# MLP second layer of a fused attention and cluster block: seven quarter products in place of eight, their sums on GpSimd, the first layer's sums in the scores' banks

## The chip, the cores and the metric

One NeuronCore of a Trainium2 chip runs the whole program. The metric is the device time of one execution in microseconds (us). All data is float32. TensorE makes each float32 product in two passes, so the profile counts two MATMUL records, and two weight loads (PEld), for each product in the code.

## The reference: what is computed

There are four images of 256 channels by 64 x 64 = 4096 pixels. Each goes through two layers.

Layer 0 is self-attention over the 4096 pixels: `q` and `k` have 32 channels, `v` has 256, `attn = softmax(q k)`, and `x = gamma * (v attn^T) + x`.

Layer 1 is a cluster block: a group norm over the whole image, two 1x1 convolutions to 96 channels, a similarity of each pixel to four centres in each fold, and a projection back to 256 channels that is added to x. Then comes the part that matters here:

```
hdn = conv1x1(group_norm(y), mlp_w1, mlp_b1)           # 256 -> 1024 channels
hdn = conv1x1(gelu(hdn), mlp_w2, mlp_b2)               # 1024 -> 256 channels
y   = y + ls2 * hdn
z   = relu(batch_norm(y * dw_w))
out = relu(batch_norm(conv1x1(z, pw_w)))               # 256 -> 256 channels
```

## The kernel before, in words

**Stages.** For each image b the program writes attention's `weighting` (64 units of 128 x 4 key rows against 512 pixels; `sc` are the scores, `av` the sums with v), then `cluster`, then `mlp`. The order of the instructions on each engine is that of the code: nothing is reordered, and only waits on data and on buffers decide when an instruction starts. Work of the next image fills gaps: its projections (vp, kp, qp) fill `cluster`, and eight of its scores are made inside `mlp`, one in each block, since ScalarE must copy them out of their banks.

**Banks.** TensorE writes to eight banks of 512 columns. Pool `ps_s` has two pairs of banks (tag "s": scores, pw, and others), `ps_a` two single banks (a0, a1: the sums of the second layer), `ps_m` two single banks (tag "m"). A tile that takes a bank waits until all that read the tile before it there are done.

**MLP.** Line 1118 on. An image's 4096 pixels are eight blocks of 512 (`blocks`; image 2 does seven here and leaves the last one to be done as filling work in image 3's cluster stage, `late_block`). A block has four steps j. `first(nb, j)` makes 2 x 128 hidden rows (rows j and j + 4 of 128, called lo and hi) for 512 pixels from 2 x 128 input rows, which are 2 x 2 quarters times 2 x 2 quarters. It does so with **seven** products of 256 columns (Winograd's form of Strassen's scheme) and seven sums: products A, abcd, CD, bac, B, D, bcd (called by their weights, line 1197), sums `plus` by VectorE from the bank and the tile `hs` (line 1233), a copy of A's product by ScalarE (line 1236), gelu by ScalarE (line 1226). The factors of the input are made by `norm`: two scalings by VectorE (line 1146) and four sums by GpSimd (lines 1159 to 1163). `hs` has four quarters of 128 x 256: h1 and h2 are lo for the first and second half of the pixels, h3 and h4 are hi.

`second(nb, acc, hs, j)` adds the second layer's part of step j: four products of 512 columns (line 1204) into the banks a0 and a1, that is **eight** quarter products. It is a generator: `mo(n)` in the following `first` draws n of its products between the products of the first layer, so the products of step j are issued in step j + 1.

After a block's last step, `finish` adds the two banks to y, scaled (VectorE, line 1277), and puts the relu of each half (ScalarE, line 1267) on the list `hooks`, which `hook()` empties in the next `first`, after the first sum. `last`, after step j = 1 of the next block, makes the closing layer's product pw (line 1173) in a pair of banks, and its two output activations (line 1183) are hooked into the step after. A score (line 359) is made after step j = 2: the copy of its first half (line 367) is issued at once, that of the second half (line 368) is hooked, and its maxima (line 372, VectorE) are drawn one by one by `rest`.

**Attention.** A dictionary `at` says after which unit and quarter a score is made (`due`), with a lead of ten units. In image 0, unit 0 has two scores, before and after its last two quarters' products.

Of the kernel before, what the change touches and what calls it, by code (L numbers as in the profile page):

```python
# [8 lines left out]
F32 = mybir.dt.float32  # L9
# [4 lines left out]
P = 128  # L14
# [31 lines left out]
def attention_then_cluster_block(  # L46
# [224 lines left out]
    def attention(b, xs):  # L271
# [281 lines left out]
        def maximum():  # L553
            half["dg"] = across(0, "rden")

# [6 lines left out]
        if b:  # L562
            for i in range(6):
                del at[i, 0]
            at.update({divmod((14 * i + 10) // 5, RG): GRP + i for i in range(8)})
        else:
            at[0, 2], at[0, 0] = at[0, 0], GRP + 1

# [7 lines left out]
        def weighting(ahead, fill, early):  # L576
# [3 lines left out]
            for u in range(units):  # L580
# [15 lines left out]
                elif u == units - 1:  # L596
                    turn_mlp()
                if u == 0 and not b:
                    weigh(u, av, 0)
                    weigh(u, av, 1)  # L600
                due(u, 0)
                if p - units > 1:
                    ahead()
                if g == GRP - 1 and more:
                    exps(u + 1)
                if u or b:
                    weigh(u, av, 0)
                    due(u, 1)
                    weigh(u, av, 1)
                if nb:  # L610
# [509 lines left out]
    def mlp(b, ys, stats2, fill, nxt, blocks):  # L1120
# [10 lines left out]
        nc.gpsimd.tensor_tensor(w_bac, w_abcd, W_D, ALU.add)  # L1131
        nc.gpsimd.tensor_tensor(w_bcd, W_B, w_abcd, ALU.subtract)
        ga, gb = group_norm(b, "gn2", stats2, fill)
        fill(N)
        ob = out[b].rearrange("(k p) h w -> p k (h w)", p=P)
        pairs = {}
# [3 lines left out]
        def norm(nb, eng):  # L1140
# [17 lines left out]
            scaled(0)  # L1158
            eng.tensor_tensor(f, f, e, ALU.subtract)  # L1159
            scaled(1)  # L1160
            eng.tensor_tensor(t2, h, f, ALU.subtract)
            eng.tensor_tensor(t3, e, t2, ALU.subtract)
            eng.tensor_tensor(t4, t2, g, ALU.subtract)

# [25 lines left out]

        norm(0, nc.vector)
        if nxt:
# [3 lines left out]
        def product(out, w, j, x):  # L1196
            nc.tensor.matmul(out, w[:, j * P : (j + 1) * P], x, start=True, stop=True)  # L1197

        def second(nb, acc, hs, j):

            for i in range(2):
                jj = j + HID // P // 2 * i
                for c in range(KC):
                    yield nc.tensor.matmul(  # L1204
                        acc[c],
                        w2_s[:, jj, c * P : (c + 1) * P],
                        hs[:, i],
                        start=(j == 0 and i == 0),
                        stop=(j == HID // P // 2 - 1 and i == 1),
                    )  # L1210

        def first(nb, j, todo):
# [5 lines left out]
            h1, h2, h3, h4 = quarters(hs)  # L1218
            u = ps_m.tile([P, NB], F32, tag="m", name=f"hu_{b}_{nb}_{j}")[:, :HB]
            p = ps_m.tile([P, NB], F32, tag="m", name=f"hp_{b}_{nb}_{j}")[:, :HB]  # L1220
            q = ps_s.tile([P, 2, NB], F32, tag="s", name=f"hq_{b}_{nb}_{j}")[:, 0, :HB]
            act = AF.Gelu_apprx_tanh
# [4 lines left out]

            def mo(n):
                for _ in range(n):
                    next(todo, None)  # L1230

            def plus(dst, ps, term):
                nc.vector.tensor_tensor(dst, ps, term, ALU.add)  # L1233

            product(p, W_A, j, e)
            nc.scalar.copy(h1, p)  # L1236
# [3 lines left out]
            rest(2 if nb == blocks - 1 and j == 3 else 1)  # L1240
            mo(1)
            product(q, W_CD, j, f)
            product(u, w_bac, j, t3)
            plus(h3, u, h2)
            product(p, W_B, j, g)
            plus(h4, q, h3)
# [3 lines left out]
            gelu(h1, h1, lo)  # L1250
            mo(1)
            product(u, W_D, j, t4)
            plus(h3, u, h3)
            gelu(h3, h3, hi)
            if nb == blocks - 1 and j == 3:
                rest(1)
            mo(1)
            product(q, w_bcd, j, h)
            plus(h2, q, h2)
            gelu(h2, h2, lo)  # L1260
            rest(1)
            mo(1)
            return hs

        def finish(nb, acc):
            def relu(c):
                nc.scalar.activation(  # L1267
                    pairs[nb][:, 1, c, :],
                    block(ys, c, nb),
                    AF.Relu,  # L1270
                    scale=dw_d[:, c : c + 1],
                    bias=dw_e[:, c : c + 1],
                )

            for c in range(KC):
                yb = block(ys, c, nb)
                nc.vector.scalar_tensor_tensor(
                    yb, acc[c], par("ls2", c), yb, ALU.mult, ALU.add
                )
                hooks.append(lambda c=c: relu(c))  # L1280


        hooks, maxima = [], []

# [7 lines left out]

        acc, todo = None, iter(())

# [4 lines left out]
        for nb in range(blocks):  # L1299
            for j in range(4):  # L1300
                hs = first(nb, j, todo)
                if j == 0:
# [5 lines left out]
                    ]  # L1308
                if nxt and (nb, j) in at:
                    nxt.score(at[nb, j], hooks, maxima)  # L1310
                if j == 1:
                    if nb:
                        last(nb - 1)
                    if nb + 1 < blocks:
                        norm(nb + 1, nc.gpsimd)
                todo = second(nb, acc, hs, j)
        for _ in range(2):
# [129 lines left out]
```

## Time and profile before

| | us |
|---|---|
| median of three runs | 3419.96 |
| lowest and highest run | 3417.59, 3421.48 |
| profiled execution | 3419.29 |
| its span in the profile | 3417.5 |
| image 0's MLP in the trace | 660 to 911 |
| one MLP block with a score, image 0 | 30.91 |
| one MLP block without a score, image 3 | 29.25 |

Lines of the profile are read so: line of the code, engine, operation, output <- inputs, shapes, number; then busy us in all and mean ns of one; then the engine's idle time ahead of it and what ended it. Lines of the timeline give start and duration in us, with "xN" for N like instructions in a row. PE is TensorE's multiplying, PEld its weight loading, DVE VectorE, ACT ScalarE, POOL GpSimd, SP the queue that issues most DMAs.

### The profile page before, as it was taken

To read this page: it belongs to the slowest core of one execution; us is meant where nothing else is said; L and a number is where in the kernel's file an instruction comes from. 1 tells how busy PE (TensorE), PEld (TensorE's weight loads), DVE (VectorE), ACT (ScalarE), POOL (GpSimd) and SP (SyncE) were. 2 spreads that over 40 slices of the span, in tenths; PEclk is the share of its full clock that TensorE was granted. 3 is DMA by queue.
4 is the path that set the end of the run, shared out by engine and by line. 5 is a ranking of instruction groups with operands and counts; after the bars stand their busy time and mean duration, and the time that the engine had idled before them with its cause. 6 is when DMAs were issued, how large, how long until landed. Compare 5 with 4: busy or idle time off the path is not lost.

```text
span 3417.5 us, 31890 instructions
## 1 busy us (share of the span) xinstructions
PE 3363.0 (98%) x11536; PEld 1663.4 (49%) x11536; DVE 2069.2 (61%) x3219; ACT 1674.2 (49%) x2157; POOL 1490.3 (44%) x807
## 2 busy tenths in 40 slices
PE   8999999999999999999999999999999999999999
PEld 4434445665533444565544344466554343445565
DVE  4667764655566766464556676646546766765543
ACT  5555543444555554344455555434446555544444
POOL 2655665210265666521125566652004675672200
PEclk9999999999999999999999999999999999999999
DMA  2000002000000000100000000010000000010000
GB/s 71 13 13 10 16 7 85 7 19 13 19 13 13 13 13 22 70 7 19 19 16 13 10 13 13 22 70 7 19 19 13 13 13 13 13 36 1 13 19 25
DMA packets 41501, 70.01 MB, mean 20 GB/s; under 512 B 9632, under 2 KB 16896, under 8 KB 41344
## 3 DMA queue, kind: packets, MB, share of 16 engines
q1 hardware_dynamic: 36480, 61.16, 5.3%
q10 hardware_dynamic: 4608, 6.30, 0.8%
q8 instruction: 91, 1.49, 0.2%
q0 software_dynamic: 256, 0.52, 0.1%
q14 instruction: 66, 0.54, 0.1%
HBM read 42.68 MB, written 16.89 MB: 17 GB/s over the span
## 4 chain that ended last, share of the span: by engine, by line
PE 95%; DVE 3%; ACT 1%; issue 0%; DMA 0%; SPq 0%; ACTq 0%; DVEq 0%
PE av L473 53%; PE mo L1204 12%; PE sc L359 8%; PE hu L1197 4%; PE pw L1173 3%; PE hp L1197 3%; PE hq L1197 3%; PE vp L310 2%; PE fv L859 2%; PE op L980 1%; PE qp L329 0%; PE kp L287 0%; DVE vf L868 0%; DVE hs L1233 0%; PE agg L889 0%
## 5 line engine op out<-in xcount | busy, mean ns | idle before, releaser
L473 PE MATMUL av<-s,v 128*128 128x512 f32 x4096 | 1820.5, 598 | 0.6 <-ACT s L463 0.6
L468 POOL TENSOR_TENSOR acc<-acc,s 128x1024 f32<-128x1024 f32 x448 | 1057.3, 2360 | 543.2 <-ACT s L463 524.4
L473 PEld LDWEIGHTS av<-s,v 128*128 128x128 f32 x4096 | 759.8, 190 | 1045.4 <-issue 1035.4
L463 ACT ACTIVATE s<-s 128x1024 f32<-128x1024 f32 x512 | 540.1, 1057 | 592.7 <-DVE s L460 549.7
L460 DVE TENSOR_TENSOR s<-s,mb 128x1024 f32<-128x1024 f32 x512 | 595.5, 1205 | 17.8 <-ACT mb L444 15.9
L1204 PE MATMUL mo<-hs,w 128*128 128x512 f32 x992 | 508.3, 595 | 3.8 <-ACT hs L1226 1.6
L381 DVE TENSOR_TENSOR top<-sc,top 128x1024 f32<-128x1024 f32 x196 | 239.4, 1221 | 377.9 <-PE sc L359 377.8
L1226 ACT ACTIVATE hs<-hs,pv_s 128x256 f32<-128x256 f32 x496 | 251.4, 508 | 361.1 <-DVE hs L1233 350.1
L1233 DVE TENSOR_TENSOR hs<-hu,hs 128x256 f32<-128x256 f32 x372 | 157.7, 424 | 356.2 <-ACT hs L1236 205.5
L377 ACT COPY s<-sc 128x1024 f32<-128x1024 f32 x224 | 224.8, 1004 | 228.8 <-PE sc L359 228.8
L1159 POOL TENSOR_TENSOR xn<-xn 128x256 f32<-128x256 f32 x27 | 23.9, 884 | 682.4 <-DVE xn L1146 488.0
L359 PE MATMUL sc<-q,k 32*128 32x512 f32 x2048 | 294.4, 640 | 3.0 <-ACT s L382 3.0
L384 DVE TENSOR_TENSOR top<-sc,top 128x1024 f32<-128x1024 f32 x196 | 240.0, 1224 | 72.6 <-ACT s L377 59.4
L382 ACT COPY s<-sc 128x1024 f32<-128x1024 f32 x224 | 227.0, 1014 | 66.2 <-DVE top L379 36.1
L465 POOL TENSOR_TENSOR acc<-s 128x1024 f32<-128x1024 f32 x32 | 75.3, 2354 | 366.8 <-ACT s L463 366.7
L1233 DVE TENSOR_TENSOR hs<-hq,hs 128x256 f32<-128x256 f32 x372 | 146.3, 421 | 107.5 <-PE hq L1197 103.2
L1204 PEld LDWEIGHTS mo<-hs,w 128*128 128x128 f32 x992 | 186.9, 190 | 42.6 <-ACT hs L1236 7.8
L359 PEld LDWEIGHTS sc<-q,k 32*128 32x128 f32 x2048 | 81.8, 182 | 193.7 <-issue 141.5
L1197 PE MATMUL hp<-xn,w 128*128 128x256 f32 x496 | 150.6, 385 | 2.6 <-ACT v L318 2.6
L1197 PEld LDWEIGHTS hp<-xn,w 128*128 128x128 f32 x496 | 92.4, 190 | 73.0 <-issue 62.5
L310 PE MATMUL vp<-wv_s,x 128*128 128x256 f32 x512 | 123.4, 387 | 0.2 <-ACT v L318 0.2
L1173 PE MATMUL pw<-xn,wpw_s 128*128 128x512 f32 x248 | 112.0, 594 | 3.4 <-ACT xn L1267 2.2
(219 smaller groups left out, 2737.7 us busy)
## 6 DMA issues: line engine op xcount, KB each, us to landing
x<-in_x SPq DMA_DIRECT2D x32, 512.0 KB, 6.6
out<-xn SPq DMA_DIRECT2D x62, 256.0 KB, 2.1
w<-in_w SPq DMA_DIRECT2D x8, 1024.0 KB, 10.2
mr<-row_mx SPq DMA_DIRECT2D x28, 256.0 KB, 3.1
rden<-row_rd SPq DMA_DIRECT2D x28, 256.0 KB, 3.1
q<-q ACTq DMA_DIRECT2D x96, 64.0 KB, 2.0
mix<-in_wfv SPq DMA_DIRECT2D x8, 192.0 KB, 8.1
q<-q SPq DMA_DIRECT2D x24, 64.0 KB, 2.0
```

Source lines behind the costliest of these rows:

```text
L359: nc.tensor.matmul(halves[r // 2][:, r % 2, :], k_s[rows, g, :], q_s[rows, :], start=True, stop=True)
L381: nc.vector.tensor_tensor(top, halves[1], top, ALU.max)
L382: nc.scalar.copy(s[:, 2:4, :], halves[1])
L384: nc.vector.tensor_tensor(top, halves[0], top, ALU.max)
L460: nc.vector.tensor_tensor(sh, sh, mxs[nb].unsqueeze(1).to_broadcast([P, 2, NB]), ALU.subtract)
L463: nc.scalar.activation(sh, sh, AF.Exp)
L468: nc.gpsimd.tensor_tensor(acc, acc, s[:, 2 * h : 2 * h + 2], ALU.add)
L473: nc.tensor.matmul(av[c], own["v"][:, RG * g + quarter, c * P : (c + 1) * P], slots[u][:, quarter, :], start=(g == 0 and quarter == 0), st ...
L1197: nc.tensor.matmul(out, w[:, j * P : (j + 1) * P], x, start=True, stop=True)
L1204: yield nc.tensor.matmul(acc[c], w2_s[:, jj, c * P : (c + 1) * P], hs[:, i], start=(j == 0 and i == 0), stop=(j == HID // P // 2 - 1 and i ...
L1226: nc.scalar.activation(dst, src, act, bias=bias)
L1233: nc.vector.tensor_tensor(dst, ps, term, ALU.add)
```

## The change

**Second layer.** In all blocks but an image's last, `second_by_seven` takes the place of `second`. It treats w2 as 2 x 2 quarters (a11, a12, a21, a22: 128 rows of step j or j + 4 by 128 output channels) and hs as the four quarters above. It makes seven products of 256 columns a step; I call them X0, X1, Y, Z0, Z1, W0, W1 after the banks that they are summed in (x is a0, y is a1, z and w are the two `ps_m` banks; 0 and 1 are a bank's halves). X0 (a12 by h3), X1 and Y (a11 by h1) take hs as it is or, for X1, weights that are sums. Between X1 and Y, and between Y and Z0, **GpSimd** makes four sums in place: h4' = h2 + h4, h2' = h2 - h1, h1' = h1 - h4', h3' = h1' + h3; Z0, Z1, W0, W1 take these in this order.

**Weights.** GpSimd makes the four sums of w2's quarters once an image (w7, a21 in place, s2, w3). Since a21 is overwritten, a DMA on SP loads that quarter again before the last block.

**End of a block.** x is final once X1 and X0 are done in step 3's set: `early` copies half of y's bank (ScalarE) and updates y (VectorE) within the next block's step j = 0. `finish` then does three 256 operations at once (d4, d3, y3) and hands four more (d2, y4, y0, y1; two of 256, two of 512) and the two relus to the list `drips`, of which each `plus` of step j = 1 issues one. An extra `hook()` in step j = 1, after the gelu of h3, issues the relus.

**First layer.** Its sums no longer go to `ps_m`: a step takes a pair of banks of `ps_s` four times (for A and abcd; CD and bac; B and D; bcd).

**Order.** The number of second-layer products at each of five places in `first` is (0, 2, 2, 1, 2), after a score (2, 2, 1, 1, 1), in the last block (0, 1, 1, 1, 1). The factors' four GpSimd sums are issued behind the h sums of step j = 1.

**Elsewhere.** The maxima's diagonal (`across`) goes to the buffer "t" instead of "rden", which the weights take. In image 0 the first seven of the scores are spread: one each seven quarters, none next to another, in place of two in unit 0 and then one a unit.

```diff
-            at[0, 2], at[0, 0] = at[0, 0], GRP + 1
+            for i in range(6):
+                del at[i, 0]
+            at.update({divmod(3 * i + 2, RG): GRP + 1 + i for i in range(7)})
...
+        nc.gpsimd.tensor_tensor(w7_s, a21_s, a11_s, ALU.subtract)
         ga, gb = group_norm(b, "gn2", stats2, fill)
         fill(N)
+        nc.gpsimd.tensor_tensor(a21_s, a21_s, a22_s, ALU.subtract)
+        nc.gpsimd.tensor_tensor(s2_s, a21_s, a11_s, ALU.subtract)
+        nc.gpsimd.tensor_tensor(w3_s, s2_s, a12_s, ALU.add)
...
+        def second_by_seven(nb, acc, hs, j):
+            h1, h2, h3, h4 = quarters(hs)
+            one, end = j == 0, j == h_n - 1
+            x, y, z, w = acc
...
+            yield q(x, 0, a12_s, h3, one)
+            yield q(x, 1, w3_s, h4, stop=end)
+            nc.gpsimd.tensor_tensor(h4, h2, h4, ALU.add)
+            nc.gpsimd.tensor_tensor(h2, h2, h1, ALU.subtract)
+            yield q(y, 0, a11_s, h1, one, end)
+            nc.gpsimd.tensor_tensor(h1, h1, h4, ALU.subtract)
+            nc.gpsimd.tensor_tensor(h3, h1, h3, ALU.add)
+            if end:
+                early(nb, acc)
+            if behind:
+                behind.pop()()
+            yield q(z, 0, w7_s, h4, one)
+            yield q(z, 1, a21_s, h2, stop=end)
+            yield q(w, 0, s2_s, h1, one)
+            yield q(w, 1, a22_s, h3, stop=end)
+
+        def early(nb, acc):
+            yb = block(ys, 0, nb)
+            nc.scalar.copy(quarters(pairs[nb][:, 1])[0], acc[1][:, :HB])
+            nc.vector.scalar_tensor_tensor(yb, acc[0], par("ls2", 0), yb, ALU.mult, ALU.add)
...
             def plus(dst, ps, term):
                 nc.vector.tensor_tensor(dst, ps, term, ALU.add)
-
+                if drips:
+                    drips.pop(0)()
+
+            mo()
             product(p, W_A, j, e)
             nc.scalar.copy(h1, p)
             product(u, w_abcd, j, t2)
             plus(h2, u, h1)
             hook()
             rest(2 if nb == blocks - 1 and j == 3 else 1)
-            mo(1)
+            mo()
+            ps = ps_s.tile([P, 2, NB], F32, tag="s", name=f"hq_{b}_{nb}_{j}")
+            q, u = ps[:, 0, :HB], ps[:, 1, :HB]
             product(q, W_CD, j, f)
             product(u, w_bac, j, t3)
             plus(h3, u, h2)
+            ps = ps_s.tile([P, 2, NB], F32, tag="s", name=f"hr_{b}_{nb}_{j}")
+            p, u = ps[:, 0, :HB], ps[:, 1, :HB]
             product(p, W_B, j, g)
             plus(h4, q, h3)
             plus(h2, q, h2)
             gelu(h4, h4, hi)
             plus(h1, p, h1)
             gelu(h1, h1, lo)
-            mo(1)
+            mo()
             product(u, W_D, j, t4)
             plus(h3, u, h3)
             gelu(h3, h3, hi)
+            if j == 1:
+                hook()
...
+            sum_(d4, p6, d1)
+            sum_(d3, p7, d4)
+            scaled(y3, p4, 1)
+            drips.append(lambda: sum_(d2, p5, d4))
+            drips.append(lambda: scaled(y4, p5, 1))
+            drips.append(lambda: scaled(y0, own[:, 0], 0))
+            drips.append(
+                lambda: scaled(
+                    y1.rearrange("p (x n) -> p x n", x=2),
+                    d3.unsqueeze(1).to_broadcast([P, 2, HB]),
+                    1,
+                )
+            )
             for c in range(KC):
+                drips.append(lambda c=c: hooks.append(lambda: relu(c)))
...
+                    else:
+                        nc.sync.dma_start(
+                            out=a21_s,
+                            in_=w2.rearrange("(k p) m -> p k m", p=P)[:, :h_n, P:],
+                        )
...
+                        behind.append(norm(nb + 1, nc.gpsimd))
```

## The prediction, on record before the changed kernel was run

> **What bounds the kernel now.** I read the page first: the shares by engine and the chain that ended last.
>
> ```profile
> PE 3363.0 (98%) x11536; PEld 1663.4 (49%) x11536; DVE 2069.2 (61%) x3219; ACT 1674.2 (49%) x2157; POOL 1490.3 (44%) x807
> PE 95%; DVE 3%; ACT 1%; issue 0%; DMA 0%; SPq 0%; ACTq 0%; DVEq 0%
> L1204 PE MATMUL mo<-hs,w 128*128 128x512 f32 x992 | 508.3, 595 | 3.8 <-ACT hs L1226 1.6
> ```
>
> TensorE is busy 98% of the span and is 95% of the chain, so fewer matmuls shorten the kernel unless TensorE then waits. Second, the timeline of one MLP step of image 0 (TensorE's lines; start, duration):
>
> ```profile
> 803.68 0.59 PE L1197 MATMUL hu<-xn,w_abcd 128*128 128x256 f32 x2
> 804.12 1.02 PE L1204 MATMUL mo<-hs,w 128*128 128x512 f32 x2
> ...
> 808.85 1.02 PE L1204 MATMUL mo<-hs,w 128*128 128x512 f32 x2
> 809.71 0.59 PE L1197 MATMUL hp<-xn,w 128*128 128x256 f32 x2
> 810.14 0.59 PE L1197 MATMUL hu<-xn,w_abcd 128*128 128x256 f32 x2
> ```
>
> Start to start, a product of 256 columns (two passes) takes 0.43 us, one of 512 columns 0.86: exactly linear, nothing per matmul. A step (seven 256s of the first layer, four 512s of the second) is 7 x 0.43 + 4 x 0.86 = 6.45, and 803.68 to 810.14 is 6.46. The closing layer's (pw) groups start every 29.25 us in image 3, which is 4 x 6.45 + 3.44: no wait at all. In image 0 they start 30.91 apart; with the scores' 1.07 the sum is 30.31, so 0.60 is lost there. Third, the pace of the helpers and the order at a block's end:
>
> ```profile
> 785.54 1.40 DVE L1277 SCALAR_TENSOR_TENSOR x<-mo,pc_s,x 128x512 f32<-128x512 f32 x2
> 786.38 1.52 ACT L1267 ACTIVATE xn<-x,dw_e,dw_d 128x512 f32<-128x512 f32 x2
> 792.10 3.60 PE L1173 MATMUL pw<-xn,wpw_s 128*128 128x512 f32 x8
> ...
> 798.77 0.76 DVE L1233 TENSOR_TENSOR hs<-hq,hs 128x256 f32<-128x256 f32 x2
> 799.45 0.41 DVE L1233 TENSOR_TENSOR hs<-hp,hs 128x256 f32<-128x256 f32 x1
> 803.31 1.01 ACT L367 COPY s<-sc 128x1024 f32<-128x1024 f32 x1 [1.01 <-PE sc L359]
> ```
>
> Now the relus (L1267) end at 787.9 and pw starts at 792.10: four us of slack. Back to back, VectorE's 256 sums start 0.34 apart (798.77, two, then 799.45), its 512 updates 0.66 apart (1.40 for two of 0.74).
>
> **What the Trainium skill says.** "ScalarE: Activation LUTs", What ACT_TABLE_LOAD costs, says that back-to-back ACTIVATEs overlap by about 93 ns: two relus of 0.80 take 1.52 here, 0.08 of overlap; it agrees. "GPSIMD Engine Reference", Specifications, says that GpSimd shares its SBUF interface with VectorE and contends with VectorE instructions in a two-port mode or with two SBUF inputs. The trace agrees: the same 128x256 sum on GpSimd takes 884 ns on average in L1159, which runs beside L1146 on VectorE, and 723 alone.
>
> ```profile
> L1159 POOL TENSOR_TENSOR xn<-xn 128x256 f32<-128x256 f32 x27 | 23.9, 884 | 682.4 <-DVE xn L1146 488.0 <-ACT hs L1226 194.4
> L1163 POOL TENSOR_TENSOR xn<-xn 128x256 f32<-128x256 f32 x27 | 19.5, 723 | 0.0
> ```
>
> "TensorE: Matmul & The Clock Gate", Part 1, says that an idle window lowers the array's clock. The stage table agrees (columns: stretch, length, busy of PE, PEld, DVE, ACT, POOL, clock, DMA): after the idle stretch of 61 to 70 us the clock is 0.79.
>
> ```profile
> 61.00:70.00 9.00, 5.49 (x18) 2.25 (x20) 5.86 (x5) 7.25 (x8) 5.35 (x3) 1.00 0.00 0
> 70.00:78.00 8.00, 8.00 (x25) 3.08 (x24) 5.08 (x6) 4.44 (x5) 3.02 (x2) 0.79 0.00 1
> ```
>
> **Part 1, the products.** All blocks but an image's last: 7 + 7 + 6 + 7 = 27 blocks, 4 steps each, 108 steps. Eight quarters of 0.43 become seven: 6.45 to 6.02, in all 108 x 0.43 = 46.4 us off TensorE. This is the whole gain of the idea; the rest is what it makes TensorE wait for.
>
> **Part 2, the block's end (the main cost).** Instead of two updates of y by VectorE, there are at step j=0's end three 256 operations, then four more (two 256, two 512) that drip in after the sums of step j=1, and only then the relus, behind the gelu of h3. I lay step j=1 out from its first product at 0. The bac product starts at 2.15 and can be read 0.64 later (800.69 to 801.33 for another one), at 2.80. From there VectorE has, in order, h3, y4, h4, y0, h2, y1, h1, h3: 5 x 0.34 + 0.38 + 2 x 0.66 = 3.40, plus the last one's 0.08 tail: 6.28. ScalarE: gelu h1 from 5.99, gelu h3 from 6.45, relu 0 from about 6.93, done at 7.74; TensorE's pw can start at 7.85 (0.06 to 0.2 after the release, as at other waits). Its own work ends at 6.02, so **1.83 us are lost per block**; bcd's wait for its banks (0.4) lies inside. Behind pw in TensorE's queue stand the next step's products, and all three helpers wait for those, so nothing makes the time good. Against that the 0.4 goes that scored blocks lose now at the first mo after the y update. The early copy and update (0.3 and 0.66, step j=0) fall into idle time of ScalarE and VectorE; if that were gone, they would add to the same chain. Bounds: 1.5 to 2.1, from 0.02 to 0.03 more or less on each of the dozen links.
>
> **Part 3, the first layer in the scores' banks.** A step now takes four bank pairs in turn, of two that there are. After pw it needs a pair while ScalarE still reads pw's: if they rotated strictly, CD (at 1.72) would wait for the second output activation (2.6). But the trace shows that the pair whose last reader is issued first is taken:
>
> ```profile
> 68.72 1.01 ACT L382 COPY s<-sc 128x1024 f32<-128x1024 f32 x1
> 68.85 1.23 DVE L384 TENSOR_TENSOR top<-sc,top 128x1024 f32<-128x1024 f32 x1 [0.78 <-ACT s L377]
> ...
> 69.79 1.53 PE L359 MATMUL sc<-q,k 32*128 32x512 f32 x8 [2.99 <-ACT s L382]
> ```
>
> At 69.79 scores start right after the copy L382 of the previous ones' second half (ends 69.73), ahead of the end (70.08) of L384, which reads their first half. So CD takes the pair of the step's own first products, free after h2's sum: no wait (0 to 0.95). After scores, though, only the first half's pair is free in that order: the A product waits for its copy, which starts 1.23 after the scores' start and lasts 1.01 (L367 above), so 2.24 plus 0.15 = 2.39; the scores end at 1.07 and two second-layer products are put in front (0.86): 0.45 us lost per scored step. In an image's last block nothing is put in front: 1.3 lost, for four scores (one, one and two in images 0, 1, 2). In return the first step of an MLP loses its waits for u's bank: about 0.4 each.
>
> **Part 4, GpSimd's sums.** Four a step, 0.72 each alone: about 3.0 of 6.02 us. In a plain step the first can start when the X1 product has been read (1.90), giving h4' at 2.7 (needed at 3.44), h2' at 3.4 (4.30), h1' after Y's product at 4.5 (5.16), h3' at 5.3 (5.59): hidden by 0.3 at the tightest. After j=1 four factor sums (3.0 us) come ahead of the next step's first: in scored blocks the 1.07 of the scores hides them, in image 3 about 0.3 a block is lost. With contention at 0.90 each the chain no longer fits (rival C). The weights' sums (four of 128x512, 1.27 each as L1130) end before the first X1, some 7 us after the group norm: nothing, and up to 2 us an image if not. The DMA that restores w2's quarter waits on SP for the last Z1, with nothing urgent behind it; its product is the last of the next step, about 6 us on: nothing.
>
> **Part 5, image 0's first scores.** The 3.0 us in which TensorE waits (66.8 to 69.79) goes, since a score is no longer next to another; with it the slow clock of 70 to 78 us, 0.21 of 8 us, 1.7. Between 3.0 and 4.7; I take 4.7. The other buffer for the maxima's diagonal, and the last block's order of products: nothing, since their inputs are a step old.
>
> **The sum.** Scored blocks with a block's end in them (6 + 6 + 5 = 17): now 30.91; then 4 x 6.02 + 3.44 + 1.07 + 1.83 + 0.45 + the 0.2 lost around scores now too = 31.07: +0.16 each, +2.7. Image 3's six: 27.52 + 1.83 + 0.3 = 29.65 against 29.25: +2.4. First blocks: -1.72 - 0.4, +0.45 in three: -7.1. Last blocks, which save nothing: 1.43 in three, 1.83 in image 3, 1.3 x 4 for the scores: +11.3. MLP +9.3, attention -4.7: +4.6. The profiled execution took 3419.29 (span 3417.5; 0.7 below the median of 3419.96): **3423.9 us**, that is nothing that can be told from no change. Measurement tells about 0.2%, 6.8 us, from no change.
>
> **The rivals.** A, my forecast: gain and waits cancel (within 0.2%). B, *faster*: the block's end costs 0.8 in place of 1.83, because the dozen links from bac's product to the relu follow each other 0.08 closer than I lay them out (an update of SBUF data on VectorE may be quicker than L1277's 0.66 from a bank): 27 x 1.0 off, 3397. For it: VectorE is only half busy in these stages, and y0 and y1 read no bank. Against: L674, which reads none either, takes 752 ns. C, *slower*: GpSimd's sums meet VectorE's two-input operations (y0, y1, the maxima) and last 0.90 as L1159's median of 895 does. Then the four need 3.6 + links, W1 waits 0.3 in each of some 100 steps: +30, 3454. It decides from about 0.83 us a sum. For it: L1159; against: only a few of a step's operations have two SBUF inputs. D, *slower*: pairs rotate strictly: CD waits 0.95 after each of 27 pw's and 0.47 after 20 scores: +35, 3459. Against it: 69.79 above.
>
> **Chances.** A 0.37, B with smaller gains of its kind 0.30, C and D with smaller mixtures of both 0.33. The range leaves out one tenth on each side: 3399 to 3447. A's own range is 3413 to 3430.
>
> **What would show it.** Right: about 46 us less PE busy time but the same span; pw's group started by the relu after 1.5 to 2.1 us idle; hp behind L367's copy by 0.45; 61 to 78 us without idle time. Wrong: pw starts at once (B); idle PE ahead of the last products put down to POOL (C); hq idle behind the output activations (D); a gap at the first second-layer product of an image (weights late).

## The result and the profile after

The changed kernel is slower. Its median is 3639.84 us (four runs, 3638.07 to 3651.35) against 3419.91 us (3417.59 to 3421.48) for the kernel before: a ratio of 1.0651, 95% interval 1.0628 to 1.0674, some 220 us more. In the experiments below, the two or three numbers in brackets behind a time are this ratio to the kernel before, measured again beside each run, and its interval. The prediction was 3423.9 us, "nothing that can be told from no change". The profiled execution took 3651.35 us (span 3649.6), the highest of the four, so the two traces differ by 232.1 us and not by 220.

From the page of the changed kernel: the busy time by engine, the chain that ended last, and three groups of matmuls (busy, mean ns | idle time ahead of them and what ended it).

```profile
PE 3416.6 (94%) x12184; PEld 1787.1 (49%) x12184; DVE 2164.1 (59%) x3381; ACT 1679.3 (46%) x2184; POOL 1834.7 (50%) x1255
...
PE 86%; DVE 10%; ACT 2%; issue 1%; DMA 0%; POOL 0%; SPq 0%; ACTq 0%; POOLq 0%; DVEq 0%
...
L1211 PE MATMUL hr<-xn,w 128*128 128x256 f32 x496 | 166.4, 418 | 111.3 <-DVE hs L1282 111.3
L1233 PE MATMUL mo<-hs,w 128*128 128x256 f32 x864 | 266.0, 390 | 0.0
L1211 PE MATMUL hp<-xn,w_abcd 128*128 128x256 f32 x248 | 89.2, 442 | 69.0 <-ACT hs L1288 62.3
```

TensorE falls from 98 to 94% of the span and from 95 to 86% of the chain; VectorE rises from 3 to 10%. The second layer's products (L1233) wait for nothing. The waits are in the first layer: the product D (tile hr, after B) waits for VectorE's sums (L1282), and abcd (tile hp, after A) for ScalarE's copy (L1288): 173.6 us together, where the page of before has no such row.

The timeline of a plain step of image 0, the lines around the two products (L1211), shows what they wait for:

```profile
729.19 0.59 PE L1211 MATMUL hp<-xn,w 128*128 128x256 f32 x2
...
729.88 0.37 ACT L1288 COPY hs<-hp 128x256 f32<-128x256 f32 x1
...
730.30 0.70 PE L1211 MATMUL hp<-xn,w_abcd 128*128 128x256 f32 x2 [0.52 <-ACT hs L1288]
...
733.89 0.41 DVE L1282 TENSOR_TENSOR hs<-hr,hs 128x256 f32<-128x256 f32 x1
...
734.36 0.70 PE L1211 MATMUL hr<-xn,w 128*128 128x256 f32 x2 [0.34 <-DVE hs L1282]
```

A starts at 729.19. Its sum p is copied by ScalarE from 729.88 to 730.25, and only then abcd starts, although abcd writes to u, the other bank of the pair. In the same way D, which writes to u, starts after VectorE has read B's sum p (733.89 to 734.30). A to abcd takes 1.11 us where it took 0.43; the idle record shows 0.52 of these 0.68 (the rest lies under the 0.59 us that a product's records last), and after such a wait the next product comes 0.54 later and not 0.43. So a wait costs its idle time and 0.27 more. A plain step takes 7.44 us (729.19 to the next A at 736.63), not 6.02.

The step that finishes a block (j = 1), VectorE's operations (L1282 the step's sums, L1355 the y updates), D, the relus and pw:

```profile
740.54 0.47 DVE L1355 SCALAR_TENSOR_TENSOR x<-mo,pc_s,x 128x256 f32<-128x256 f32 x1
...
740.93 0.41 DVE L1282 TENSOR_TENSOR hs<-hq,hs 128x256 f32<-128x256 f32 x1
...
741.26 1.18 DVE L1355 SCALAR_TENSOR_TENSOR x<-xn,pc_s,x 128x512 f32<-128x512 f32 x1
...
742.37 0.41 DVE L1282 TENSOR_TENSOR hs<-hq,hs 128x256 f32<-128x256 f32 x1
742.70 0.87 DVE L1355 SCALAR_TENSOR_TENSOR x<-xn,pc_s,x 128x512 f32<-128x512 f32 x1
743.50 0.41 DVE L1282 TENSOR_TENSOR hs<-hr,hs 128x256 f32<-128x256 f32 x1
...
743.96 0.70 PE L1211 MATMUL hr<-xn,w 128*128 128x256 f32 x2 [2.50 <-DVE hs L1282]
...
745.57 1.50 ACT L1327 ACTIVATE xn<-x,dw_e,dw_d 128x512 f32<-128x512 f32 x2
746.43 0.70 PE L1187 MATMUL pw<-xn,wpw_s 128*128 128x512 f32 x1
```

Here VectorE's queue holds the block's end between the sums, so D waits 2.50 us. Of D's 124 waits 29 are over 1 us; they hold 69.2 of its 111.3 us. Of the 24 longest, 12 are also followed by a slower array: in the stage table (stretch, length, busy of PE, PEld, DVE, ACT, POOL, clock, DMA) the clock is 0.57 in the 4 us after the wait of the block before, and 1.00 after the one shown above; the last section says what tells the two kinds apart.

```profile
61.00:70.00 9.00, 8.80 (x25) 3.72 (x26) 6.18 (x6) 6.93 (x8) 5.66 (x3) 1.00 0.00 0
70.00:78.00 8.00, 8.00 (x25) 3.15 (x24) 6.55 (x10) 5.52 (x6) 6.14 (x3) 1.00 0.01 3
700.00:705.00 5.00, 2.49 (x13) 1.86 (x11) 3.90 (x8) 0.60 (x2) 3.23 (x4) 1.00 0.00 0
705.00:709.00 4.00, 4.00 (x11) 3.23 (x12) 1.62 (x4) 2.73 (x5) 0.00 (x0) 0.57 0.00 0
744.00:748.00 4.00, 3.96 (x14) 2.63 (x15) 1.76 (x4) 2.77 (x5) 0.00 (x0) 1.00 0.00 0
```

The trace's clock record holds 103.2 us at half speed against 27.3 before. The first two lines are image 0's first scores: no idle stretch and no slow clock, as predicted.

**Where the 232 us are.** This is an estimate from the figures above. Products saved: -46.4. Idle time of abcd and D: 173.6. 0.27 for each of their 244 waits: 65.9. Half of the additional 75.9 us at half speed: 38. Sum 231. It is no exact balance (slow stretches overlap waits, and there are smaller terms of both signs), but nothing of size is left over.

### The profile page after: what moved, and what is told of

The parts are those of the page before. It is cut to its first block, busy times and chain, and to the rows that moved or that the text cites. A ratio compares the mean times of both kernels' runs of the same rounds, so it can differ in the third digit from the quotient of the medians.

```text
span 3649.6 us, 33984 instructions
## 1 busy us (share of the span) xinstructions
PE 3416.6 (94%) x12184; PEld 1787.1 (49%) x12184; DVE 2164.1 (59%) x3381; ACT 1679.3 (46%) x2184; POOL 1834.7 (50%) x1255
## 4 chain that ended last, share of the span: by engine, by line
PE 86%; DVE 10%; ACT 2%; issue 1%; DMA 0%; POOL 0%; SPq 0%; ACTq 0%; POOLq 0%; DVEq 0%
PE av L473 49%; PE sc L359 8%; PE mo L1233 7%; DVE hs L1282 5%; PE hp L1211 4%; PE pw L1187 3%; PE hq L1211 3%; PE hr L1211 3%; PE vp L310 2%; PE fv L857 2%; DVE x L1355 2%; PE ht L1211 2%; ACT hs L1288 1%; PE mo L1217 1%; PE op L978 1%
## 5 line engine op out<-in xcount | busy, mean ns | idle before, releaser
L1239 POOL TENSOR_TENSOR hs<-hs 128x256 f32<-128x256 f32 x108 | 78.3, 725 | 560.2 <-PE mo L1233 548.2
L1211 PE MATMUL hr<-xn,w 128*128 128x256 f32 x496 | 166.4, 418 | 111.3 <-DVE hs L1282 111.3
L1233 PE MATMUL mo<-hs,w 128*128 128x256 f32 x864 | 266.0, 390 | 0.0
L1282 DVE TENSOR_TENSOR hs<-hp,hs 128x256 f32<-128x256 f32 x124 | 52.6, 424 | 315.6 <-PE hp L1211 315.5
L1282 DVE TENSOR_TENSOR hs<-hq,hs 128x256 f32<-128x256 f32 x372 | 148.0, 419 | 130.3 <-PE hq L1211 126.7
L1233 PEld LDWEIGHTS mo<-hs,w 128*128 128x128 f32 x864 | 167.6, 196 | 38.8 <-issue 15.2
L1211 PEld LDWEIGHTS hr<-xn,w 128*128 128x128 f32 x496 | 86.5, 194 | 174.1 <-DVE hs L1282 167.1
L1282 DVE TENSOR_TENSOR hs<-hr,hs 128x256 f32<-128x256 f32 x248 | 103.8, 419 | 85.0 <-PE hr L1211 81.4
L1211 PE MATMUL hp<-xn,w_abcd 128*128 128x256 f32 x248 | 89.2, 442 | 69.0 <-ACT hs L1288 62.3
```

Source lines behind the costliest of these rows:

```text
L1233: return nc.tensor.matmul(bank[:, half * HB : (half + 1) * HB], a[:, j], t, start=start, stop=stop)
```

## The theories

1. The two sums of a pair are one tile, and the program lets a product into one half wait for every earlier-issued read of the other half.
2. VectorE's queue, lengthened by a block's end, is late, and D is the first to feel it.
3. GpSimd's sums hold up the second layer (rival C of the prediction).

## Experiments: the order of products and reads

If theory 1 holds, it is enough to issue each of the two products ahead of the read that it waits for. The kernel with both moved:

```diff
-            nc.scalar.copy(h1, p)
             product(u, w_abcd, j, t2)
+            nc.scalar.copy(h1, p)
...
-            plus(h1, p, h1)
-            gelu(h1, h1, lo)
             mo()
             product(u, W_D, j, t4)
+            plus(h1, p, h1)
+            gelu(h1, h1, lo)
```

> The changed kernel with two products moved: abcd is issued ahead of ScalarE's copy of p, and D ahead of VectorE's sum of h1 with p. Theory 1 (the two sums of a pair are one tile, and a product into one half of it waits for every earlier read of the other half): the 124 waits of abcd (0.52 us idle each and 0.27 of tail and restart) and of D (111 us idle in all and 0.27 each) go, 240 us, and most of the slow clock that follows the 2.5 us waits; the block's end comes back as a wait of pw of about 1.8 us in 27 blocks, so some 3,425 us (3,405 to 3,450). The copy of p then starts only after abcd, the mirror of the same rule. Theory 2 (VectorE's queue, longer by the block end's operations, is simply late, and D is the first to feel it): the wait moves to the next product that reads or frees, at least 3,590. Theory 3 (GpSimd's sums hold the second layer's products): no change, 3,640.

Measured: 3469.19 us (ratio to before 1.0151, 1.0136 to 1.0166), 170.7 less than the changed kernel. abcd waits for the copy no more, and D once in all (2.8 us). Theory 3 falls, and so does theory 2 as the cause of these waits: nothing was taken from VectorE's or GpSimd's work. The timeline of this kernel, A's and abcd's products and the copy (now L1289), shows the mirror of the wait:

```profile
716.98 0.59 PE L1211 MATMUL hp<-xn,w 128*128 128x256 f32 x2
...
717.41 0.59 PE L1211 MATMUL hp<-xn,w_abcd 128*128 128x256 f32 x2
...
718.09 0.37 ACT L1289 COPY hs<-hp 128x256 f32<-128x256 f32 x1 [0.38 <-PE hp L1211]
```

Before, the copy began 0.69 after A's start (729.19 to 729.88). Now it begins 0.68 after abcd's (717.41 to 718.09), though it reads only A's sum. The pair is ordered as one thing, for reads after writes too. The median is still 44 above the 3,425 expected, and above the range given. The trace has four places for it: CD waits for h2's sum, which is late with the copy (TensorE's weight loads for it 28.0 us in 49 steps); pw waits 33.2 us in 30 places and bcd, at the block's end too, 12.1 in 24; and the first products of an image wait 14.3 for VectorE. The block's end and the start of an image are taken up below.

Each move alone, the first and then the second half of that diff:

> Only abcd ahead of the copy of p. Theory 1: 124 times (0.52 + 0.27) us less, 98, so about 3,542, with D's waits as they are. Theory 2: under 20 us less, since VectorE stays the late one: 3,620 or more. Theory 3: 3,640.

Measured: 3582.23 us (1.0482, 1.0467 to 1.0498), 57.6 less than the changed kernel, where 98 were expected. abcd's 62.3 us are gone, but the copy comes later, so h2's sum and with it the release of the pair that CD takes: TensorE's weight loads for CD (tile hq) wait 28.0 us in 49 steps for VectorE, 1.9 in 4 before. That is the mirror's price, and the slow clock is 9 us longer as well.

> Only D ahead of the sum of h1 with p. Theory 1: 111 us of idle time and 124 times 0.27 go, and up to 38 us of slow clock; about 50 come back as pw's wait at the block's end: 3,505 (3,460 to 3,530). Theory 2: 3,590 or more. Theory 3: 3,640.

Measured: 3540.59 us (1.0359, 1.0342 to 1.0377), 99 less. D's 111.3 us shrink to 2.7, and the slow clock from 103 to 51. Of this, pw takes back 33.2 us of idle time in 30 waits and bcd 12.5 in 25. Direction and kind are those of theory 1; the gain is below the range expected, since more came back at the block's end.

Last, only the layout without the seven products: the kernel before, with its first layer's sums put in the scores' pairs, and one call of hook() between a score and pw, which the banks need.

```diff
-            u = ps_m.tile([P, NB], F32, tag="m", name=f"hu_{b}_{nb}_{j}")[:, :HB]
-            p = ps_m.tile([P, NB], F32, tag="m", name=f"hp_{b}_{nb}_{j}")[:, :HB]
-            q = ps_s.tile([P, 2, NB], F32, tag="s", name=f"hq_{b}_{nb}_{j}")[:, 0, :HB]
+            ps = ps_s.tile([P, 2, NB], F32, tag="s", name=f"hp_{b}_{nb}_{j}")
+            p, u = ps[:, 0, :HB], ps[:, 1, :HB]
...
                 if j == 1:
+                    if nxt and (nb, j) in at:
+                        hook()
```

> The kernel before, with its eight quarter products, old block end, old order, and only the first layer's sums put in the scores' pairs of banks as in the changed kernel. Theory 1: the same two waits appear here, 124 times (0.79 for abcd, at least 0.61 for D), about 174 us more than before: 3,594 (3,560 to 3,620). Theory 2: within 10 us of before, as the longer queue at a block's end is not there. Theory 3: within 10 us of before.

Measured: 3620.91 us (1.0591, 1.0575 to 1.0607), 202.6 more than before and just above the range expected. Its page has the same two rows:

```profile
L1197 PE MATMUL hr<-xn,w 128*128 128x256 f32 x496 | 160.6, 406 | 51.1 <-DVE hs L1232 51.1
...
L1197 PE MATMUL hp<-xn,w_abcd 128*128 128x256 f32 x248 | 86.3, 430 | 67.0 <-ACT hs L1235 66.3
```

So both waits come with the place of the first layer's sums; they need neither the seven products nor GpSimd's sums nor the new block's end. Their size does depend on the block's end: without it, D's idle time is 51.1 us and not 111.3, only four of its waits are over 1 us (29 in the changed kernel), and the clock is at half speed for 41.4 us and not 103.2. So about 60 us of waits, and half of the 62 us of slow clock, need both: the order inside a pair, and a VectorE that is late with the read. That much of theory 2 stands. Another 25.8 us (23 waits) is A waiting for the copy of a score's first half, since nothing is put ahead of A here; the changed kernel, with two products ahead, has 3.4 us of it, in last blocks.

## Experiments: GpSimd beside VectorE

With both products moved, a block of image 0 takes 32.33 us; 4 x 6.02 + 3.44 + 1.07 would be 28.59. A part of the rest is at the block's end, where y0 and y1 took 1.18 and 0.87. In this kernel GpSimd's four sums were left out:

```diff
-            nc.gpsimd.tensor_tensor(h4, h2, h4, ALU.add)
-            nc.gpsimd.tensor_tensor(h2, h2, h1, ALU.subtract)
...
-            nc.gpsimd.tensor_tensor(h1, h1, h4, ALU.subtract)
-            nc.gpsimd.tensor_tensor(h3, h1, h3, ALU.add)
```

> The kernel with both products moved, without GpSimd's four sums of h (they are left out, so that the second layer takes h as it is). In the run before, the y0 and y1 updates at a block's end took 1.18 and 0.87 us, where the prediction had taken 0.66 each. Theory 1 (GpSimd beside them makes these two-input updates of SBUF data slow, and they stand in the chain to pw): 0.73 us less in each of 27 blocks, 20 us: 3,449. Theory 2 (they are that slow by themselves): 3,469. Theory 3 (TensorE also waits for GpSimd's sums in many steps): below 3,440, with the difference in the steps that have no block's end.

Measured: 3456.02 us (1.0107, 1.0092 to 1.0123), 13.2 less than with the sums (14.3 if each is set against its own measurement of the kernel before). The y0 and y1 updates, first with, then without GpSimd's sums (groups, number | busy, mean ns):

```profile
L1355 DVE SCALAR_TENSOR_TENSOR x<-xn,pc_s,x 128x512 f32<-128x512 f32 x54 | 52.8, 977 | 0.0
```

```profile
L1351 DVE SCALAR_TENSOR_TENSOR x<-xn,pc_s,x 128x512 f32<-128x512 f32 x54 | 40.1, 743 | 0.0
```

12.7 us shorter, and 13.2 us gained: theory 1 of that run, at two thirds of the 20 us expected. With the sums, VectorE's next operation comes 1.11 and 0.80 after y0 and y1 start, in 22 of the 27 blocks; in the other five no sum of GpSimd runs beside them, and it comes after 0.66 each, as in all 27 without the sums. 22 x 0.59 are 13.0 us, about the whole gain. This is what "GPSIMD Engine Reference", Specifications, of the Trainium skill says of two SBUF inputs. The prediction used it for GpSimd's time alone; the trace shows that both engines pay. GpSimd's fourth sum takes 1.05 us beside these updates (at 741.98 in the changed kernel) and 0.73 in the median, but no product waits for it there, while VectorE's updates stand in the chain to pw.

The same at an image's start, where the prediction had put nothing. The trace of the changed kernel: GpSimd's weight sums (L1142, L1143), VectorE's gb (L260) and the first block's two scalings (L1156), and the first product:

```profile
654.71 1.26 POOL L1142 TENSOR_TENSOR w<-w 128x512 f32<-128x512 f32 x1
654.78 1.21 DVE L260 SCALAR_TENSOR_TENSOR gb_gn<-ga_gn,dv_gn,pc_s 128x2 f32<-128x2 f32 x1
...
656.02 2.97 DVE L1156 TENSOR_SCALAR xn<-x,ga_gn,gb_gn 128x512 f32<-128x512 f32 x2
656.05 1.26 POOL L1143 TENSOR_TENSOR w2s<-w 128x512 f32<-128x512 f32 x1
...
657.65 1.22 PE L1211 MATMUL hp<-xn,w 128*128 128x256 f32 x2 [2.82 <-DVE xn L1156]
```

In the kernel before, where no weight sum runs then, the same steps:

```profile
659.12 0.22 DVE L260 SCALAR_TENSOR_TENSOR gb_gn<-ga_gn,dv_gn,pc_s 128x2 f32<-128x2 f32 x1
...
659.38 0.55 DVE L1146 TENSOR_SCALAR xn<-x,ga_gn,gb_gn 128x512 f32<-128x512 f32 x1
```

An operation on two numbers a partition takes 1.21 us and ends with GpSimd's (654.71 + 1.26 = 655.97). The trace of before had such a case, which the prediction did not read:

```profile
656.47 1.27 POOL L1132 TENSOR_TENSOR w_bcd<-w,w_abcd 128x512 f32<-128x512 f32 x1
656.66 1.09 DVE L246 SCALAR_TENSOR_TENSOR mv_gn<-dv_gn,mv_gn 128x1 f32<-128x1 f32 x1
```

L246 runs eight times there: four times beside a weight sum, where it takes 0.95 to 1.10 us and ends with it, and four times with GpSimd idle, where it takes 0.22. A later run moves the sums at the image's start.

## Experiment: the scores alone

The kernel before with nothing but the changed order of image 0's scores, and unit 0's quarters in the same order as every other unit's:

```diff
-            at[0, 2], at[0, 0] = at[0, 0], GRP + 1
+            for i in range(6):
+                del at[i, 0]
+            at.update({divmod(3 * i + 2, RG): GRP + 1 + i for i in range(7)})
```

> The kernel before with nothing but image 0's first seven scores spread as in the changed kernel. The forecast's part 5: 4.7 us less than before (3.0 of wait, 1.7 of slow clock), 3,413.6. By the trace of the changed kernel, in which image 0's MLP starts at 657.65 in place of 660.02: 2.4 less. A rival: nothing, because the later scores come too late and give back the time.

Measured: 3415.06 us against 3419.48 (0.9988, 0.9981 to 0.9994): 4.4 less, by the interval 2 to 6.5. The forecast's 4.7 lies within that, and so does 2.4; no gain at all does not. The changed kernel's MLP starts only 2.4 earlier because the 2 us lost at its image start lie ahead of that mark.

## Experiments: a version that keeps the gain

First, the block's end was given a step's time. The core of the edit, on the kernel with both products moved (the second layer's products are spread anew as well):

```diff
-            at = {(u, 2): u for u in range(GRP)}
+            at = {(u, 3): u for u in range(GRP)}
...
-                if j == 1:
+                if j == 2:
...
                     if nb:
                         last(nb - 1)
                     if nb + 1 < blocks:
-                        behind.append(norm(nb + 1, nc.gpsimd))
+                        norm(nb + 1)
...
+            drips.append(begin)
+            drips.append(lambda: scaled(1))
+            drips.append(lambda: factor(0, nc.vector))
+            drips.append(lambda: factor(1, nc.vector))
+            drips.append(lambda: [factor(i, nc.gpsimd) for i in (2, 3)])
```

> The kernel with both products moved, and the block's end given time: pw comes after step j=2 in place of j=1, the scores after j=3, the norm of the next block by VectorE's sums of step j=3 (two of its four factor sums on VectorE); three second-layer products in place of two between abcd and CD after pw, and three ahead of A after a score. If what is left of the loss is the chain of the block's end (1.21 us of pw's wait, 0.52 of bcd's, 0.27 each of tail and restart) and the banks after pw and scores (0.52 and 0.27 each): a block of image 0 falls from 32.33 to 28.8, of image 3 from 30.28 to 27.7, 17 times 3.5 and 6 times 2.6, 75 us: 3,394, faster than before. Rival: the chain moves along (the factors of the next block are now the late ones, and abcd waits for them): 3,440 to 3,470.

Measured: 3483.45 us (1.0187, 1.0173 to 1.0201), 14 more than with pw after j = 1, and above both ranges expected. The rival was right in kind, as the wait moved along, but to bcd and not to abcd. pw waits for a relu once, but the extra operations on VectorE now stand ahead of the sum of h2 with q, which frees the pair that bcd takes. From its waits (us, times, longest):

```profile
PE ht L1219 <- DVE hs L1288: 41.1, 53, 1.0
```

So they were put where no release stands behind them, in groups of one to three (one score of the last block and the last maximum also move behind):

```diff
             plus(h2, u, h1)
             hook()
+            drip()
...
             plus(h4, q, h3)
             plus(h2, q, h2)
+            drip()
...
             gelu(h2, h2, lo)
+            drip()
```

> As in the run before (pw after step j=2), but the extra VectorE operations no longer stand between the step's own sums that free a pair of banks: they are issued after the first sum and the hooks, after the sum of h2 with q, and at the step's end. In the run before, bcd waited 41.1 us in 53 steps for the h2 sum that frees q's pair, with one or two extra operations ahead of it in VectorE's queue. Theory (a bank's release is on TensorE's path, so what stands ahead of the releasing sum is what costs): those waits go, 41.1 + 53 times 0.27 = 55 us, and some 10 of slow clock, so 3,415 (3,395 to 3,435), about the time of before. Rival (VectorE has too much to do in these steps, wherever it stands): the waits move to D's or the next A's and the time stays within 20 us of 3,483.

Measured: 3433.32 us (1.0045, 1.0028 to 1.0062), 50 less: bcd's waits fall to 6.4 us in 18 steps. The theory holds: within its range, though short of the expected 3,415.

Then the weights' sums and the last small moves, as two kernels. In the first, the last factor sum of an image's first block goes to GpSimd as well:

```diff
-        nc.gpsimd.tensor_tensor(a21_s, a21_s, a22_s, ALU.subtract)
-        nc.gpsimd.tensor_tensor(s2_s, a21_s, a11_s, ALU.subtract)
-        nc.gpsimd.tensor_tensor(w3_s, s2_s, a12_s, ALU.add)
...
         norm(0)
+        nc.gpsimd.tensor_tensor(a21_s, a21_s, a22_s, ALU.subtract)
+        nc.gpsimd.tensor_tensor(s2_s, a21_s, a11_s, ALU.subtract)
+        nc.gpsimd.tensor_tensor(w3_s, s2_s, a12_s, ALU.add)
```

> As the run before, but three of the four weight sums of an image (GpSimd, 1.27 us each) are issued behind the first block's norm, and the last of that norm's factor sums is done by GpSimd, so that they start only when VectorE has done its part. In the runs so far VectorE's gb took 1.20 us where it took 0.22 in the kernel before, and the two scalings 2.97 where they took 1.09, both until a weight sum of GpSimd ended; the first product waited 2.82 us for them, and TensorE then ran at half clock for 6.8 us. Theory (GpSimd's two-input sums hold VectorE's operations on SBUF data): 2 us of wait and up to 3.4 of slow clock go in each of four images, 8 to 22 us: 3,418 (3,411 to 3,426). Rival (VectorE is late there for another reason, or X1 then waits for the late weights): no change, 3,430 to 3,436.

Measured: 3413.91 us (0.9981, 0.9972 to 0.9989), 19.4 less than the run before it, 4.9 an image, in the range expected. gb is back at 0.22 us, the two scalings take 1.00 in place of 2.97, and the slow clock falls from 52.4 to 21.8 us.

The second, on top of it:

```diff
-                        (3, 2, 1, 1, 0)
+                        (3, 2, 0, 1, 1)
                         if scored
-                        else (0, 3, 1, 1, 2)
-                        if j == 2 and nb
+                        else (0, 3, 1, 0, 3)
+                        if j == 2
...
-            drip()
-            rest(2 if nb == blocks - 1 and j == 3 else 1)
+            if drips:
+                drip()
+            else:
+                rest(2 if nb == blocks - 1 and j == 3 else 1)
```

> The run of the weight sums, and three small moves: W0 and W1 and Z1 behind bcd in step j=3, so that both pairs of banks are free when the score comes (0.25 us of wait and 0.27 of tail and restart in 20 steps, 10 us); the second-layer products after a score spread as 3, 2, 0, 1, 1 (the next A no longer waits 0.15 for the pair of B and D); maxima not drawn in steps that draw a block's end (bcd's 0.32 and 0.27 in 18 steps, 10 us). Theory: 3,395 (3,388 to 3,408), faster than before. Rival: VectorE's work only moves to the next release, and the time stays at that of the run beside it.

Measured: 3411.59 us (0.9974, 0.9963 to 0.9985), faster than the kernel before by 8.7 us (5 to 13 by the interval). It is 2.3 less than its neighbour and not 19, and the two intervals overlap: the rival of that run was nearer. Its timeline around a score shows what is left: no idle record, and yet starts that are 0.60, 0.54 and 0.59 apart where 0.43 is TensorE's own pace.

```profile
738.32 0.59 PE L1219 MATMUL hr<-xn,w 128*128 128x256 f32 x2
738.92 0.70 PE L1219 MATMUL ht<-xn,w_bcd 128*128 128x256 f32 x2
739.46 0.59 PE L1241 MATMUL mo<-hs,w 128*128 128x256 f32 x2
...
740.32 0.59 PE L1241 MATMUL mo<-hs,w 128*128 128x256 f32 x2
740.91 1.46 PE L359 MATMUL sc<-q,k 32*128 32x512 f32 x8
```

A block with a score takes 30.62 us (before: 30.91; without waits: 28.59), one without 28.55 (before: 29.25; without waits: 27.52). Of the 8.7 us that this version gains, the scores' new order is worth 4.4, so the seven products with all that they need bring about 4; with the two intervals that is barely told from nothing.

## Why the prediction was wrong

**Part 1 held.** A product starts 0.43 after the one before, one is gone from each of 108 steps, 46.4 us; the timeline of the last version shows 13 products in a row at that pace (749.26 to 754.44, 12 times 0.43). TensorE's busy time did not fall by 46 but rose by 53.6, since a product after a wait is recorded at 0.70 and one at half clock at over 1 us.

**Part 3 is the step that failed.** It says: "So CD takes the pair of the step's own first products, free after h2's sum: no wait (0 to 0.95)", and lets everything else in the step go at TensorE's pace. It asked which pair comes free when, from a line in which whole pairs change hands, but not what a product waits for inside a pair that the step already holds. A and abcd, B and D share a tile, and the read of the first was issued ahead of the second. The term that was missing is 0.79 a step for abcd (0.52 idle and 0.27) and 0.61 and more for D, 240 us of waits and the slow clock behind them; some 60 us of that only because VectorE is late at a block's end. In the kernel before, u, p and q lay in tiles of their own, and both products into a score's or pw's pair are issued ahead of all reads, so its trace had no such wait to read; the tiles in the diff had it. "PSUM — Partial Sum Buffer", Terms, of the Trainium skill says that two engines may not be on one bank, in the same group of 32 partitions, at a time. p and u lie in different banks, so no reason of the hardware's is seen, and the trace of before has TensorE write u while ScalarE reads p, each in a bank and a tile of its own:

```profile
795.96 0.59 PE L1197 MATMUL hu<-xn,w_abcd 128*128 128x256 f32 x2
796.22 0.37 ACT L1236 COPY hs<-hp 128x256 f32<-128x256 f32 x1 [3.81 <-PE hp L1197]
```

So the runs show an order of the program, set for the tile. That the wait goes when each bank of the pair is a tile of its own was not run.

The rest of part 3: no rotation was found in which pw's pair holds CD (rival D; its one such wait is 1.0 us with both products moved). A behind the copy after a score: about 0.2 us in a scored block (721.45 + 0.43 to 722.08) in place of 0.45, and 1.1 in three last blocks in place of 1.3 in four.

**Part 2** was right in kind and too small. In the changed kernel itself D's wait swallows it: j = 1 takes 9.80 us up to pw (736.63 to 746.43), 3.78 lost, of which 0.79 is abcd's. With both products moved it shows alone: A at 723.12, pw at 731.32, 8.20 in place of 6.02: 2.18 against 1.83, above the range of 1.5 to 2.1. The mis-sized term is y0 and y1, put at 2 x 0.66 and 1.11 + 0.80 from start to start beside GpSimd. Without GpSimd's sums the same stretch takes 7.62: 1.60 lost, inside the range, so the other links were laid out well. Rival B needed an end that costs 0.8; it was further off.

**Part 4.** GpSimd's sums are hidden: 725 to 798 ns on average, and no product of the changed kernel waits for one (its weight loads 3.6 us in all with both products moved). Rival C falls. The price that counted was on the other side, at VectorE; and the weights' sums, "nothing, and up to 2 us an image if not", cost 4.9 an image (with the move of one factor sum): in image 0, 2 us of wait (2.82 in place of 0.86) and 6.8 us at half speed behind it.

**Part 5** held within the noise (4.4, 2 to 6.5 by the interval, against 4.7).

**The range** (3399 to 3447) was built from the sizes of waits that had been thought of. Nothing in it stood for a wait of the changed layout that the trace of before could not show.

## What to carry to other kernels

When sums are moved into shared tiles, write down for each write which reads of the whole tile are issued ahead of it: issue all writes of a tile first, then its reads, and the wait is gone, at the cost of a later first read. Look at what that read frees: here the later copy held up CD. When an extra operation is put on a helper engine, look at which buffer release stands behind it, not at the engine's share. And a GpSimd operation is not free just because its engine is idle: look at what VectorE does in the same microsecond.

## What the runs showed of the hardware

- A short wait of TensorE costs more than its idle record. For products of 256 columns, 0.16 us lie under the record of the product ahead (0.59 long, 0.43 from start to start) and 0.11 are added behind (0.54 in place of 0.43), so a wait below 0.16 shows no idle time at all and still takes its time.
- Some idle times of 2.5 us were followed by stretches of 3.41 us (and multiples) at half clock. "TensorE: Matmul & The Clock Gate", Part 1, of the Trainium skill gives windows of that length and has the slow state come after an idle window of about 3.4 us; here 2.5 us of idle time ahead of 704.93 were enough (clock 0.57 in the next 4 us). What decided is where the wait lay. In the changed kernel's clock record all slow stretches start on one grid of 3.41 us, to within 0.05 (705.05 is one of its marks). Of D's 24 waits over 2.3 us, the 12 with at least 2.00 us between two marks were followed by a slow stretch, as the one ahead of 704.93; the 12 with at most 1.95 between any two neighbouring marks were not, as the one ahead of 743.96, which a mark at 742.60 cuts into 1.14 and 1.37. With abcd alone moved, D's 24 waits of this size fall the same way: 15 with 1.97 or more, 9 with 1.91 or less.
- An operation of VectorE on 128 x 2 elements, whose inputs are no larger, took 1.21 us in place of 0.22 while GpSimd added two 128 x 512 tiles, and ended with it.
